# Two graph layers, 32 batches: the product of the score weights ahead of batch 0, and Y of batch 1 directly behind O of batch 0

## The chip, the cores and the metric

The kernel runs on one core of one Trainium2 chip. The metric is the device time of one execution in microseconds; before the change it is 2266.42 us (median of 3 runs, 2264.99 to 2266.43). The engines named below: PE (TensorE, matrix products; PEld is its weight load), DVE (VectorE), ACT (ScalarE), POOL (GpSimd) and SP (SyncE, which issues nearly all DMAs). All arithmetic is fp32.

## The reference

`x` and `adj` are 32 x 512 x 512, `nodemask` 32 x 512, the layer-0 weight W is 512 x 1024, `Wqk` 512 x 1024, `Wv` 512 x 512.

```python
def _L0_gnn_ref(x, adj, W):
    deg = jnp.sum(adj, axis=-1, keepdims=True)
    agg = jnp.einsum('bij,bjf->bif', adj, x) / jnp.maximum(deg, EPS)
    cat = jnp.concatenate([x, agg], axis=2)
    return jax.nn.relu(jnp.einsum('bnf,of->bno', cat, W))

def _L1_gnn_ref(X, adj, mask, Wqk, Wv):
    q, k = jnp.split(X @ Wqk, 2, axis=-1)
    v = X @ Wv
    agg = jnp.einsum('bij,bjd->bid', adj, k * mask[:, :, None])
    w = inv_scale * mask * jnp.einsum('bid,bid->bi', q, agg)
    return jax.nn.softmax(w, axis=1)[:, :, None] * v

h = jnp.maximum(_layernorm(x, axis=-1), 0.0)
x = x + _L0_gnn_ref(h, adj, W)
h = jnp.maximum(_layernorm(x, axis=-1), 0.0)
x = x + _L1_gnn_ref(h, adj, nodemask, Wqk, Wv)
```

## The kernel before

Each batch needs five products of 512 x 512 matrices. Y = h W2 (W2 is the second half of the layer-0 weight) and O = h W1 + A Y, where A is adj divided by its row sums; X1 = x + relu(O) is the input of the second layer. h1 is the normalized X1. U = A (h1 masked), and TV is h1 times two weights at once: T, with the product M = Wq Wk^T (scaled), and V, with Wv. The scores are the row-wise dot products of T and U. M is the same for all batches: it is the "product of the score weights" of the title. Its tiles are called `pm`, its function `multiply`.

Every 512 x 512 product is done by a scheme of seven products of 256 x 256 blocks, m1 to m7 (`product`, L138). The operands are kept in seven slots: four blocks and three sums of blocks, made on DVE by `left_sums` and `right_sums`. One block product is four matmuls (eight passes on PE, since fp32 takes two), PE needs 1.73 us for it. The sums of the result are kept apart in PSUM tiles `pp`, `pr` and `pq`. `pp` takes m1 and is copied by ACT, then m6 is added on top and it is copied again, then m7, a copy, and m4. So m6 cannot start before the copy of m1's block is done, and m7 not before the copy of m6's. The usual order is m1, m2, m6, m5, m7, m3, m4; with `sooner` it is m1, m2, m5, m6, m7, m3, m4.

The order on each engine is written out by hand. `run` (L191) takes one product and a `Plan`: after each block product it issues the functions that the plan has for that step, and then the product's own copies and sums. Each engine works through its own list in this order, and waits at the head of the list.

The operand on the left must lie transposed. For most batches this is done with DMAs: `FrontH.write` (L339, the normalized h) and `FrontA.write` (L377) write a chunk of 128 rows to DRAM (`dhT`, `daT`), `Turned.read` (L311) reads it back in another order (`shT`, `saT`, two halves of four DMAs each), and DVE turns 32 x 32 squares (`Turned.turn`, L314). h1 goes the same way (`dh1T`, `sh1T`). Batch 0 has its h and A transposed on PE instead (`turn_chunk`, L788). The weights, turned on DVE, are w1R (W1's seven slots; `s1` is its raw form), w2R (W2), and wqT and wkT. w1R is written to DRAM once (`dw`, L963, 1.8 MB) and later read slot by slot (`stream`).

SP's DMAs use eight completion semaphores in turn: each DMA waits until the one issued eight before it has landed.

`start` (L829) does batch 0 up to the point where the loop takes over. Before the change its stages on PE are:

1. `spare` (L868): seven matmuls of zeros, after a first Sqrt on ACT that loads its table;
2. batch 0's h, transposed on PE, and Y_0 (`layer0_y(0)`, `sooner`);
3. O_0 (`layer0_out(0, ...)`), with the statistics and writes of h of batch 1, and the turning of Wqk, in its plan;
4. M: `multiply(0)` to `multiply(3)` with no other product beside them (`run(None, 14, p)`, L1035); the plan has what follows from O_0 (`chain`, L807: statistics, normalization, mask and write of h1 of batch 0) and the turns of h of batch 1.

Then the loop runs, for batch i: O_i (not for i = 0), TV of batch i-1, U_i, Y_(i+1). For i = 0 the loop has U_0 and Y_1 alone. So the order on PE is Y_0, O_0, M, U_0, Y_1, O_1, TV_0, U_1, Y_2, O_2 and so on.

Before TV_0 the right operand of TV (`mv`, both M and Wv) gets its own sums of slots: eight functions `weights`, four over rows (`outer`, 1024 wide) and four over columns (`inner`, 1792 wide). Under these names `place` copies a quarter of M or Wv into `mv`.

Of the kernel before, what the change touches and what calls it, by code (L numbers as in the profile page):

```python
# [11 lines left out]
F32 = mybir.dt.float32  # L12
# [10 lines left out]
def kernel(  # L23
# [10 lines left out]

# [166 lines left out]
    def half_rows(t, src, h):  # L226
        for q, rows in enumerate(by_rows(src)):
            nc.sync.dma_start(out=t[q * R:(q + 1) * R, :, :], in_=rows[:, 2 * h:2 * h + 2, :])

    def exchange(src, name, t=None):  # L230


        if t is None:
            t = big.tile([P, 8, P], F32, tag="s", bufs=2, name=name)
        for q in range(Q):
            nc.sync.dma_start(out=t[q * R:(q + 1) * R, :, :], in_=src[:, :, ts(q, P)].rearrange("k r j -> r k j"))
        return t
# [5 lines left out]
    X, AT_, DEG, W, Y, H1M, H1T, U, TV = ({} for _ in range(9))  # L243
# [30 lines left out]

    def first_variance(t):

        mv, rstd, nmr = t
        v, y, r = [small.tile([P, 2], F32, tag=n, name=n) for n in ("first_v", "first_y", "first_r")]
        nc.vector.tensor_scalar(v, mv[:, 0:2, 1], LN_EPS, None, op0=ALU.add)
        nc.scalar.activation(y, v, AF.Sqrt)  # L280
        nc.vector.reciprocal(y, y)
        nc.vector.scalar_tensor_tensor(r, y, -0.5, y, op0=ALU.mult, op1=ALU.mult)
        nc.vector.tensor_tensor(r, r, v, op=ALU.mult)
        nc.vector.scalar_tensor_tensor(rstd[:, 0:2], r, 1.5, y, op0=ALU.add, op1=ALU.mult)
# [38 lines left out]
    class FrontH:  # L323
# [20 lines left out]
        def turn(self, h):  # L344
            self.to.turn(h, hT)

        def sums(self, i):
            left_sums(of(hT))[i]()

    class FrontA:  # L350
# [31 lines left out]
        def turn(self, h):  # L382
            if h == 0:
                AT_[self.b] = slots("aT", 1, f"aT_{self.b}")
            self.to.turn(h, AT_[self.b])
# [82 lines left out]
    def layer0_y(b):  # L468
        y = Y[b] = slots("yh", 1, f"y_{b}")
        return product(f"y_{b}", [(hT, right(w2R))], *into(y), sooner=b == 0)  # L470

    def layer0_out(b, w1):
# [10 lines left out]
        return product(f"o_{b}", [(hT, w1), (AT_[b], right(Y[b]))], place, finish)  # L483
# [282 lines left out]
    def turn_rows(t, h, dst, ordered):  # L766


        t = t.rearrange("p k (a r) -> p k a r", r=R)
        if ordered:  # L770
            for q in range(2):
                o = dst.rearrange("p a (c q r) -> p q c a r", c=C, q=Q)[:, 2 * h + q]
                nc.vector.transpose(o, t[:, q * 4:(q + 1) * 4, :, :])
        else:
            nc.vector.transpose(dst[:, :, ts(h, H)].rearrange("p a (k r) -> p k a r", r=R), t)
# [31 lines left out]
    def chain(p, f, n):  # L807


        def write(c):  # L810
            f.write(c, block(f"h1_{f.b}_{c}"))

        p.at(n(2), f.keep)
        p.at(n(0), f.stats, 2)
        p.at(n(0), shift, f.t, 0, 2)
        p.at(n(0), write, 0)
        p.at(n(1), f.stats, 3)
        p.at(n(1), variance, f.t, 2, 4)
        p.at(n(1), write, 1)
        p.at(n(2), shift, f.t, 2, 4)  # L820
        p.at(n(2), f.mask, 0)
        p.at(n(2), f.mask, 1)
        p.at(n(3), write, 2)
        p.at(n(4), write, 3)
        p.at(n(4), f.mask, 2)
        p.at(n(5), f.masked_sums, 0)
        p.at(n(5), f.mask, 3)

    def start():  # L829
# [6 lines left out]
        room_x(0)  # L836
        s2 = []
        for h in range(2):
            half_rows(X[0][:, 2 * h:2 * h + 2, :], x[0], h)
        for h in range(2):  # L840
            s2.append(exchange(weight_source(w0[:, F:2 * F])[8 * h:8 * h + 8], f"sw2_{h}"))
        fa = FA[0] = FrontA(0)
        fa.load(0)
        fa.load(1)
        room = mv_tile("room").rearrange("p s i a f -> p (s i a f)")
# [4 lines left out]
        w1R = room[:, 0:3584].rearrange("p (s b f) -> p s b f", s=7, b=2)  # L850
        s1 = exchange(weight_source(w0[:, 0:F]), "sw1", rows16(3584))
        fh = FH[1] = FrontH(1)
        for h in range(2):
            fh.load(h, room[:, 9728 + 1024 * h:9728 + 1024 * (h + 1)].rearrange("p (c f) -> p c f", c=2))
        sq = exchange(weight_source(wqk[:, 0:F]), "swq", rows16(5632))
        sk = exchange(weight_source(wqk[:, F:2 * F]), "swk", rows16(7680))
# [7 lines left out]

        nc.scalar.activation(still[:, 0:1], still[:, 1:2], AF.Sqrt)
        spare = mm_tile("spare").rearrange("p a f -> p (a f)")
        for n in range(7):
            nc.tensor.matmul(spare, still[:, 0:P], still, start=True, stop=True)  # L868
# [15 lines left out]
        statistics(X[0][:, 0, :], t, 0, "0_0")  # L884
        statistics(X[0][:, 1, :], t, 1, "0_0")
        first_variance(t)
        shift(t, 0, 2)
        for c in range(2):
            normal(c)
            turn_chunk(v[c], c, "h")  # L890
        for c in range(2):
            keep_chunk(h0, c, "h")
        statistics(X[0][:, 2, :], t, 2, "0_0")
        statistics(X[0][:, 3, :], t, 3, "0_0")
        variance(t, 2, 4)
        turn_right(s2[0], 0, 0, w2R)
        shift(t, 2, 4)
        turn_right(s2[0], 0, 1, w2R)
        for k in range(2):
            turn_right(s2[1], 1, k, w2R)  # L900
        r2, l0 = right_sums(of(w2R)), left_sums(of(h0))

        a0 = AT_[0] = slots("aT", 1, "aT_0")
        rows = {}
# [8 lines left out]
        p.at(0, normal, 2)  # L913
        p.at(0, normal, 3)
# [33 lines left out]
        fb = FA[1] = FrontA(1)  # L948
        p = Plan()
        p.at(0, keep_chunk, a0, 2, "a")  # L950
        p.at(0, turn_chunk, Later(rows, 3), 3, "a")
        p.at(1, keep_chunk, a0, 3, "a")
        p.at(1, fb.load, 0)
        p.at(2, fb.load, 1)
        la = left_sums(of(a0))
        for k in range(4):
            p.at(2 + k // 2, la[k])
        for c in range(C):
            p.at(3 + c, fh.stats, c)
            p.at(7 + c, fh.write, c)  # L960
        p.at(6, variance, fh.t)
        p[7].insert(0, lambda: shift(fh.t))
        p.at(7, lambda: nc.sync.dma_start(out=stream.d.rearrange("s p b f -> p s (b f)"), in_=w1R.rearrange("p s b f -> p s (b f)")))  # L963
        for c in range(C):
            p.at(10 + c, fb.sum, c)
        p.at(7, turn_rows, sq[:, 0:8], 0, wqT, True)
        p.at(8, turn_rows, sq[:, 8:16], 1, wqT, True)
        p.at(9, turn_rows, sk[:, 0:8], 0, wkT, False)
        p.at(9, turn_rows, sk[:, 8:16], 1, wkT, False)
        p.at(10, fh.to.read, 0)  # L970
        p.at(11, fh.to.read, 1)
# [12 lines left out]
        p.at(8, mask_order)  # L984
# [3 lines left out]
        p.at(13, variance, f.t, 0, 2)  # L988
        run(layer0_out(0, right(w1R)), 14, p)


        mv = mv_tile("mv")
        p = Plan()

        def multiply(d):
            m = held["m", d] = mm_tile(f"pm_{d}")
            for a in range(C):
                nc.tensor.matmul(  # L998
# [309 lines left out]
```

## Time and profile before

| what | us |
|---|---|
| runs: lowest, median, highest | 2264.99, 2266.42, 2266.43 |
| span of the profiled execution | 2263.7 |
| batch period in the loop (from one TV to the next) | 69.5 |
| first matmul of `spare`, first needed matmul | 2.28, 11.35 |
| O_0 on PE | 28.15 to 52.77 |
| M on PE | 52.77 to 67.06 |
| U_0 on PE | 67.06 to 79.14 |
| Y_1 on PE | 79.14 to 91.23 |
| O_1 on PE | 91.23 to 115.40 |

The profile is of one execution, on the only core; its span is 2.7 us shorter than the median of the runs. Times in it are microseconds from its first instruction. A line of the timeline gives start, duration, engine, line of the kernel, operation, the tiles written and read, and in brackets how long the engine had been idle before and what ended that. A line of the busy times by stretch gives the stretch, then for PE, PEld, DVE, ACT and POOL the busy time and the number of instructions, the granted clock, the DMA share and GB/s. DMA issues are shown on the queue that issues them, and their landing is a separate figure.

### The profile page before, as it was taken

To read this page: it belongs to the slowest core of one execution; us is meant where nothing else is said; L and a number is where in the kernel's file an instruction comes from. 1 tells how busy PE (TensorE), PEld (TensorE's weight loads), DVE (VectorE), ACT (ScalarE), POOL (GpSimd) and SP (SyncE) were. 2 spreads that over 40 slices of the span, in tenths; PEclk is the share of its full clock that TensorE was granted. 3 is DMA by queue.
4 is the path that set the end of the run, shared out by engine and by line. 5 is a ranking of instruction groups with operands and counts; after the bars stand their busy time and mean duration, and the time that the engine had idled before them with its cause. 6 is when DMAs were issued, how large, how long until landed. Compare 5 with 4: busy or idle time off the path is not lost.

```text
span 2263.7 us, 32771 instructions
## 1 busy us (share of the span) xinstructions
PE 2256.1 (100%) x10498; PEld 1976.5 (87%) x10498; DVE 1913.3 (85%) x3782; ACT 1028.4 (45%) x1898; POOL 175.3 (8%) x260
## 2 busy tenths in 40 slices
PE   9999999999999999999999999999999999999999
PEld 7888888888888888888888888888888888888888
DVE  7788888888888888888888888888888888888776
ACT  4454543445434544344444344543454443445323
POOL 0000000000000000100000000001000000000000
PEclk9999999999999999999999999999999999999999
DMA  9978787887878787877878788887878787887644
GB/s 220 246 218 241 208 210 191 206 229 212 210 198 199 210 229 200 209 192 208 233 203 207 194 204 220 219 209 200 192 213 229 202 208 195 204 233 205 155 124 108
DMA packets 409644, 463.68 MB, mean 205 GB/s; under 512 B 37856, under 2 KB 271328, under 8 KB 405248
## 3 DMA queue, kind: packets, MB, share of 16 engines
q1 hardware_dynamic: 399904, 428.56, 70.1%
q0 software_dynamic: 8928, 32.51, 8.6%
q8 instruction: 83, 1.36, 0.3%
q14 instruction: 89, 0.73, 0.1%
q10 hardware_dynamic: 640, 0.52, 0.1%
HBM read 293.93 MB, written 167.51 MB: 204 GB/s over the span
## 4 chain that ended last, share of the span: by engine, by line
PE 99%; DMA 0%; DVE 0%; ACT 0%; SPq 0%; POOL 0%; issue 0%; DVEq 0%; POOLq 0%
PE ptv L502 28%; PE pp_o L129 19%; PE pp_y L129 10%; PE pp_u L129 10%; PE pq_o L129 9%; PE pq_u L129 5%; PE pq_y L129 5%; PE pr_o L129 5%; PE pr_y L129 2%; PE pr_u L129 2%; PE pw L553 1%; PE pm L998 1%; PE spare L868 0%; DMA n<-in_x_dram 0%; PE pp_v L129 0%; PE pp_t L129 0%
## 5 line engine op out<-in xcount | busy, mean ns | idle before, releaser
L502 PE MATMUL ptv<-mv,h1T 128*128 128x256 f32 x2940 | 639.8, 379 | 0.1
L502 PEld LDWEIGHTS ptv<-mv,h1T 128*128 128x128 f32 x2940 | 558.4, 190 | 76.6 <-DVE xu L481 0.7
L100 DVE TENSOR_TENSOR tv<-tv 128x256 f32<-128x256 f32 (+1 forms) x644 | 320.9, 510 | 13.1 <-ACT tv L106 1.5
L106 ACT ACTIVATE tv<-ptv 128x512 f32<-128x512 f32 (+1 forms) x360 | 185.0, 541 | 260.0 <-PE ptv L502 259.4
L129 PE MATMUL pp_y<-wide 128*128 128x256 f32 x1024 | 242.1, 379 | 0.9 <-ACT y L106 0.7
L129 PE MATMUL pp_u<-h1m,aT 128*128 128x256 f32 x1024 | 241.9, 379 | 0.0
L129 PE MATMUL pp_o<-y,aT 128*128 128x256 f32 x1024 | 241.9, 379 | 0.0
L129 PE MATMUL pp_o<-w,wide 128*128 128x256 f32 x992 | 234.3, 379 | 0.0
L129 PEld LDWEIGHTS pp_y<-wide 128*128 128x128 f32 x1024 | 194.3, 190 | 27.9 <-ACT y L106 1.1
L129 PEld LDWEIGHTS pp_u<-h1m,aT 128*128 128x128 f32 x1024 | 194.5, 190 | 26.8 <-issue 0.5
L129 PEld LDWEIGHTS pp_o<-y,aT 128*128 128x128 f32 x1024 | 194.5, 190 | 26.4
L129 PEld LDWEIGHTS pp_o<-w,wide 128*128 128x128 f32 x992 | 188.5, 190 | 25.6
L106 ACT ACTIVATE o<-pp_o 128x512 f32<-128x512 f32 x96 | 57.3, 597 | 300.4 <-PE pp_o L129 300.4
L106 ACT ACTIVATE y<-pp_y 128x512 f32<-128x512 f32 x128 | 76.4, 597 | 236.1 <-PE pp_y L129 234.9
L100 DVE TENSOR_TENSOR tv<-ptv,tv 128x512 f32<-128x512 f32 x240 | 139.6, 613 | 43.2 <-PE ptv L502 39.5
L103 DVE TENSOR_TENSOR h1T<-h1T 128x512 f32<-128x512 f32 (+1 forms) x189 | 163.4, 878 | 1.2
L106 ACT ACTIVATE xu<-pp_u 128x512 f32<-128x512 f32 x127 | 75.8, 597 | 191.9 <-PE pp_u L129 191.9
L273 POOL TENSOR_TENSOR rstd<-rstd,mhalf 128x2 f32<-128x2 f32 (+1 forms) x96 | 78.6, 818 | 647.7 <-DVE rstd L272 645.6
L129 PE MATMUL pq_u<-h1m,aT 128*128 128x256 f32 x512 | 121.1, 379 | 0.0
L129 PE MATMUL pq_y<-wide 128*128 128x256 f32 x512 | 121.0, 379 | 0.0
L129 PE MATMUL pq_o<-y,aT 128*128 128x256 f32 x512 | 120.9, 379 | 0.0
L100 DVE TENSOR_TENSOR tv<-ptv,m_tv 128x512 f32<-128x512 f32 (+1 forms) x120 | 72.1, 622 | 56.2 <-PE ptv L502 55.3
(152 smaller groups left out, 3258.9 us busy)
## 6 DMA issues: line engine op xcount, KB each, us to landing
w<-dw SPq DMA_DIRECT2D x217, 256.0 KB, 4.2
a<-in_adj_dram SPq DMA_DIRECT2D x256, 128.0 KB, 3.0
dx<-xu SPq DMA_DIRECT2D x32, 1024.0 KB, 5.0
sh1T<-dh1T SPq DMA_DIRECT2D x256, 128.0 KB, 3.3
shT<-dhT SPq DMA_DIRECT2D x248, 128.0 KB, 5.7
daT<-a SPq DMA_DIRECT2D x124, 256.0 KB, 3.0
saT<-daT SPq DMA_DIRECT2D x248, 128.0 KB, 3.3
xu<-in_x_dram SPq DMA_DIRECT2D x124, 256.0 KB, 5.4
```

Of the source, the lines that this page charges most:

```text
L100: (on or nc.vector).tensor_tensor(o, a, b, op=ALU.add)
L103: (on or nc.vector).tensor_tensor(o, a, b, op=ALU.subtract)
L106: nc.scalar.activation(o, i, AF.Copy)
L129: nc.tensor.matmul(p[:, rc, :], lt[:, LEFT[k], dk, ts(rc, P)], right[:, dk, :], start=first and rc == 0 and dk == 0, stop=True, skip_group ...
L273: nc.gpsimd.tensor_tensor(rstd[:, a:b], rstd[:, a:b], mhalf[:, a:b], op=ALU.pow)
L502: nc.tensor.matmul(banks[n][:, :, ts(i, P)], left[:, LEFT[k], LEFT_IN[j], :], mvR[:, RIGHT[k], RIGHT[j], :, :], start=first and i == 0, st ...
L553: nc.tensor.matmul(banks[n][:, ts(i, P)], left[:, LEFT[k], LEFT_IN[j], :], mvR[:, RIGHT[k], RIGHT[j], which, :], start=first and i == 0, s ...
L998: nc.tensor.matmul(m.rearrange("p a f -> p (a f)"), wqT[:, a, ts(d, P)], wkT[:, a, :], start=(a == 0), stop=(a == C - 1),)
```

## The change

- M is computed at the start, ahead of batch 0. Wq and Wk are the first loads, Wq in four pieces of 256 KB (64 KB for each DMA), Wk in two of 512 KB; x of batch 0 and W2 follow. These loads are issued alternately from SP and ACT (`two_queues`). `multiply` works on half rows (256 wide).
- `spare` has five matmuls instead of seven, and the first Sqrt on ACT and `first_variance` (which used Sqrt) are gone: the variances of batch 0 go to POOL as all others do.
- Y_1 runs directly behind O_0, with `sooner`; U_0 follows Y_1. Both move into `start`, and the loop begins with i = 1. The order on PE is M, Y_0, O_0, Y_1, U_0, O_1, TV_0 and so on.
- h of batch 1 gets its own room (`HT[1]`), in `tv`, which is unused until TV_0; w1R lies in the other half of `tv`, and Y_1 takes w1R's place once O_0 is done. A of batch 1 takes A of batch 0's buffer: its first half is turned during U_0, the second in O_1.
- The plans of these stages are written anew: in O_0 the statistics of batch 1's x come one step earlier, all four writes of its h come at steps 6 and 7, the read back at steps 8 and 9, the turns at 10 and 11; the placing of Wv and the turning of the mask are in O_0; what `chain` had spread over M's fourteen steps is in the first five of Y_1's seven. Loads and writes of adj of batch 1, x of batch 2 and adj of batch 2 move with their stages.

```diff
+        exchange(wk_rows[0:8], "swk_0", sk[:, 0:8], two_queues)
+        for d in range(C):
+            exchange(wq_rows[d], f"swq_{d}", sq[:, 4 * d:4 * d + 4], two_queues)
+        exchange(wk_rows[8:16], "swk_1", sk[:, 8:16], two_queues)
         room_x(0)
+        for h in range(2):
+            half_rows(X[0][:, 2 * h:2 * h + 2, :], x[0], h, two_queues)
...
-        nc.scalar.activation(still[:, 0:1], still[:, 1:2], AF.Sqrt)
         spare = mm_tile("spare").rearrange("p a f -> p (a f)")
-        for n in range(7):
+        for n in range(5):
...
+        for d in range(C):
+            multiply(d, 0)
+        multiply(0, 1)
+        place_m(0)
         for c in range(2):
             normal(c)
+        multiply(1, 1)
+        place_m(1)
+        multiply(2, 1)
+        for c in range(2):
             turn_chunk(v[c], c, "h")
         for c in range(2):
             keep_chunk(h0, c, "h")
+        multiply(3, 1)
...
-        return product(f"y_{b}", [(hT, right(w2R))], *into(y), sooner=b == 0)
+        return product(f"y_{b}", [(HT.get(b, hT), right(w2R))], *into(Y[b]), sooner=b < 2)
...
         for c in range(C):
-            p.at(3 + c, fh.stats, c)
-            p.at(7 + c, fh.write, c)
-        p.at(6, variance, fh.t)
-        p[7].insert(0, lambda: shift(fh.t))
+            p.at(2 + c, fh.stats, c)
+            p.at(6 + c // 2, fh.write, c)
+        p.at(5, variance, fh.t)
+        p[6].insert(0, lambda: shift(fh.t))
         p.at(7, lambda: nc.sync.dma_start(out=stream.d.rearrange("s p b f -> p s (b f)"), in_=w1R.rearrange("p s b f -> p s (b f)")))
+        p.at(7, mask_order)
+        p.at(8, mask_turn)
+        p.at(9, mask_keep)
+        p.at(8, fh.to.read, 0)
+        p.at(9, fh.to.read, 1)
         for c in range(C):
+            p.at(8 + c, lambda c=c: place(c, 1, wvN[:, c, :]))
             p.at(10 + c, fb.sum, c)
-        p.at(7, turn_rows, sq[:, 0:8], 0, wqT, True)
-        p.at(8, turn_rows, sq[:, 8:16], 1, wqT, True)
-        p.at(9, turn_rows, sk[:, 0:8], 0, wkT, False)
-        p.at(9, turn_rows, sk[:, 8:16], 1, wkT, False)
-        p.at(10, fh.to.read, 0)
-        p.at(11, fh.to.read, 1)
+        p.at(10, fh.turn, 0)
+        p.at(11, fh.turn, 1)
+        for k in range(4):
+            p.at(11 + (k + 1) // 2, fh.sums, k)
         f = F1[0] = FrontH1(0)
         p.at(12, f.stats, 0)
         p.at(12, f.stats, 1)
         p.at(13, variance, f.t, 0, 2)
+        p.at(13, weights[0])
         run(layer0_out(0, right(w1R)), 14, p)
+        Y[1] = w1R
         p = Plan()
+        p.at(0, f.stats, 2)
+        p.at(0, shift, f.t, 0, 2)
+        p.at(0, write, 0)
+        p.at(0, f.stats, 3)
+        p.at(0, variance, f.t, 2, 4)
+        p.at(1, write, 1)
+        p.at(1, shift, f.t, 2, 4)
+        p.at(1, f.keep)
+        p.at(1, f.mask, 0)
+        p.at(1, f.mask, 1)
+        p.at(2, write, 2)
+        p.at(2, write, 3)
+        p.at(2, weights[1])
+        p.at(3, f.mask, 2)
+        p.at(3, f.mask, 3)
...
+        p.at(5, fb.write, 0)
+        p.at(5, fb.write, 1)
...
+        run(layer0_y(1), 7, p)
+        fh = FH[2] = FrontH(2)
+        p = Plan()
+        p.at(0, fb.write, 2)
+        p.at(0, fb.write, 3)
+        p.at(0, f.turn, 0)
+        p.at(1, f.turn, 1)
+        for n in range(4):
+            p.at(0, stream.load)
+        p.at(1, fb.to.read, 0)
+        p.at(2, fh.load, 0)
+        p.at(2, fh.load, 1)
+        p.at(3, fb.to.read, 1)
+        p.at(3, load_x, 1)
...
+        for c in range(C):
+            p.at(3 + c, fh.stats, c)
+        p.at(4, fb.turn, 0)
...
+        run(layer1_u(0), 7, p)
...
+            if i == 1:
+                p.at(0, FA[1].turn, 1)
+                for k in (0, 2):
+                    p.at(0, FA[1].sums, k)
```

## The prediction

> **What bounds the kernel now.** I read the page's engine shares and chain first, then the timeline of PE at the start, the busy times by stage, the timeline around the hand-over from one stage to the next, and last the landing times of single DMAs.
>
> ```profile
> PE 2256.1 (100%) x10498; PEld 1976.5 (87%) x10498; DVE 1913.3 (85%) x3782; ACT 1028.4 (45%) x1898; POOL 175.3 (8%) x260
> ...
> PE 99%; DMA 0%; DVE 0%; ACT 0%; SPq 0%; POOL 0%; issue 0%; DVEq 0%; POOLq 0%
> ```
>
> TensorE (PE) is the chain. There are two places where time can be won: PE time that does no needed work, and gaps. The timeline of PE shows both at the very start:
>
> ```profile
> 2.28 9.23 PE L868 MATMUL spare<-late 128*128 128x512 f32 x14 [2.28 <-ACT late L865]
> 11.35 1.04 PE L792 MATMUL h<-late,h 128*128 128x128 f32 x8
> 12.63 1.99 PE L129 MATMUL pp_y<-wide 128*128 128x256 f32 x8 [0.25 <-ACT wide L106]
> ...
> 21.55 1.99 PE L129 MATMUL pp_y<-wide 128*128 128x256 f32 x8 [0.69 <-ACT y L106]
> ```
>
> The first needed matmul starts at 11.35; `spare` multiplies zeros. The 0.69 at 21.55 is m7 waiting until ACT has copied m6's sum out of the same PSUM tile, because `sooner` puts m6 directly in front of m7. The waits of PE from 12 to 130 us are these 0.25 and 0.69 alone. By stage (PE, PEld, DVE, ACT, POOL):
>
> ```profile
> 28.15:52.77 24.62, 24.62 (x119) 21.68 (x118) 20.48 (x38) 9.32 (x19) 1.02 (x1) 1.00 1.13 245
> 52.77:67.06 14.29, 14.29 (x38) 6.32 (x37) 8.54 (x20) 8.65 (x14) 1.39 (x2) 1.00 0.85 278
> ...
> 91.23:115.40 24.17, 24.17 (x113) 21.28 (x112) 23.89 (x32) 8.26 (x18) 0.00 (x0) 1.00 0.69 182
> ```
>
> These are O_0, the weight product `pm`, and O_1. In the middle one DVE works 8.54 of 14.29: this product is the cover under which the hand-over from O_0 to U_0 runs (statistics of X1, its normalization, the transposed h of batch 1). O_1 has no room on DVE. What runs under that cover:
>
> ```profile
> 46.51 0.40 SPq L963 DMA_DIRECT2D dw<-room  x1
> ...
> 54.68 1.52 ACT L294 ACTIVATE h<-xu,nmr,rstd 128x512 f32<-128x512 f32 x2 [4.47 <-DVE nmr L288]
> ...
> 55.84 4.02 SPq L236 DMA_DIRECT2D shT<-dhT  x8
> ...
> 63.02 1.25 DVE L316 STREAM_TRANSPOSE wide<-shT 128x1024 f32<-128x1024 f32 x1 [1.48 <-DMA shT<-dhT]
> ```
>
> h of batch 1 is ready in hT only at 64.3, 11.5 us after O_0's end, and nobody minds: Y_1 starts at 79.14. DVE waits for both `shT` halves (this is the second), ACT's first write of X1's h waits 4.47 for DVE's shift. The time from issue to landing of `dw`, and then of the `dhT` write behind it (issued at 47.01), each asked for alone:
>
> ```profile
> DMA to landing us min/median/max: 7.3/7.3/7.3
> ...
> DMA to landing us min/median/max: 8.8/8.8/8.8
> ```
>
> So `dw` (1.8 MB) lands at 53.85, and a 256 KB write issued 0.5 us after it lands at 55.8: it queues behind it. The `dhT` write issued before `dw` lands at 45.91 + 3.7 = 49.6, so `dw` moves for 4.2 us.
>
> **What the Trainium skill says.** (1) "DMA: Bandwidth & Descriptors", section "Queues, rings and completion order": each DMA engine consumes descriptors in ring order, SP and ACT have rings on the same 16 engines. The trace agrees (dw and dhT above), so two issuing queues save issue time but no transfer time. (2) "TensorE: Matmul & The Clock Gate", Part 1: the array runs at half clock until about one busy window has passed. Here: `spare` passes come every 0.855 us until 8.3, then every 0.43, 6.0 us after the first. (3) Same page, section "Architectural detail": the queues of ACT and DVE are strictly first in, first out; both timelines agree. (4) "ScalarE: Activation LUTs", "What ACT_TABLE_LOAD costs": about 1283 ns; the trace has 1.28 at 0.73.
>
> **The change part by part.**
>
> *Head.* Without the Sqrt, `spare` waits for DVE's memset, done at 1.42, and starts at 1.45 instead of 2.28. Five matmuls are ten passes: 7 at 0.855 and, after 6.0 us, 3 at 0.43: end 8.75. The weights come first now. In the trace the first of the 128 KB loads lands at 0.73 + 2.1 = 2.9 and the sixteenth at 7.88 + 4.7 = 12.6: 0.65 us per 128 KB. Wqk (2 MB) is then in at about 12.7, x at 17.5, W2 at 22.5, a at 27.5, s1 at 33. Each piece of Wq is turned about 1.5 us before its matmuls, so PE runs from 8.75. `pm` costs the same 32 passes (13.85 = 14.29 less 0.43 of mask transposes): eight half groups of 1.73, plus 0.87 for the first h transposes: Y_0 starts at 8.75 + 13.85 + 0.87 = 23.5. ACT must be in time: its last DMA issue waits for x (17.3), then 0.45, table load 1.28, place 0.6, two normals 1.6: 21.25, and the transpose of chunk 1 is due at 21.35. Just enough; a later ACT costs its lateness. Y_0 at 12.63 plus 13.85 would be 26.5: **3.0 gained**. Bounds: clock change a microsecond earlier or later, weights 1 to 3 later: 0 to 3.7. Y_0's further inputs all move by about 10 us as the PE does.
>
> *Hand-over, on the clock of before (O_0 at 28.15).* Wqk's turns (4.84 of DVE) leave O_0; its DMA no longer stands before wvN and adj of batch 1. Statistics come a step earlier but behind DVE's same queue, so shift ends at 41.0. ACT normalizes four chunks, 0.8 each, to 44.1. The four `dhT` writes go out as they come; the last is issued at 44.15 and lands 2.0 later (an unqueued `daT` write needs 2.0), at 46.2. `dw`, issued at 44.5, follows for 4.2: 50.4. Both `shT` reads queue behind it, 8 x 0.65: the halves land at 53.0 and 55.6. PE finishes O_0 at 52.77 + 0.43 = 53.2 and now wants them.
>
> But Y_1's start is not what ends last. On ACT, write(0) of X1 stands in front of the copy of Y_1's first block, and m6 (and with `sooner` m7) reuses that PSUM tile. write(0) needs shift of X1, and on DVE these stand before it: second turn 1.25, sum 0.65, O_01's two 1.42, two sums 1.3, two statistics 1.74, sum 0.65, variance 0.2, weights[0] 1.2, O_10 0.7, statistics 0.85, shift 0.15: 10.1, from 55.6. With write 0.8 and copy 0.6, m6 may start at 67.1 instead of 58.4. From that copy to the copy of m6's block ACT has write(1) 0.76, two masks 1.33, two writes 1.52, m5's copy 0.6, two masks 1.33, the copy 0.6: 6.15, so m7 at 73.3. Three blocks of 1.727: U_0 at 78.5. Without waits Y_1 (12.09, from 53.2) would end at 65.3: **13.2 lost**. Bounds: if the reads don't queue behind dw, DVE starts the turns at 48.2 (end of O_11's pair) and U_0 starts at 48.2 + 1.25 + 10.1 + 1.4 + 6.15 + 5.2 = 72.3: 7.0 lost; with a slower tail of dw, 15.
>
> *U_0, O_1.* SP has adj writes of batch 1, which wait for ACT behind Y_1's last copy, then 1 MB of w, saT, then x of batch 2. The last are about 12 us of queue behind Y_1's end, and DVE's statistics of x stand in front of the turn of aT that O_1 needs. From there DVE works without a pause to O_1's last xu add: 32.4 us by the rows of before (9.6 up to the aT sums, 8.3 for h1T and O_00, 14.8 for weights, O_11, O_01, statistics), 0.3 before O_1's start. In before that add starts at
>
> ```profile
> 119.42 0.68 DVE L481 SCALAR_TENSOR_TENSOR xu<-pp_o,xu 128x512 f32<-128x512 f32 x1
> ```
>
> and ends 28.9 after O_1's start, when the second product of TV wants its PSUM tile; 32.1 is **3.3 lost** (0 to 6). From batch 2 on, both kernels are the same.
>
> *Edits with one answer.* w1R, then Y_1, and h of batch 1 lie in tv, unused until TV_0: same shapes, no cost. first_variance (Sqrt) gives way to POOL's power (0.25 + 0.74 after the variance), under `pm`. wvN's placings (0.6 each) go from U_0 into O_0, where ACT is busy 9.32 of 24.62; the mask's transposes (0.43 of PE) move too. aT of batch 1 shares aT_0's buffer: its first turn runs beside U_0, its second (1.25, two sums 1.3) comes after it, and is in O_1's sum above. If ACT's slack in O_0 were gone, the dhT writes would slip by as much.
>
> Sum: -3.0 + 13.2 + 3.3 = +13.5. The profiled execution spans 2263.7, the runs' median is 2266.4, 2.7 more; the same distance after: 2277.2 and **2280 us**.
>
> **The rivals.** A: the reads pass dw, or land early; DVE and ACT order alone remain: -3.0 + 7.0 + 3.3 = +7.3, 2274; with nothing lost in O_1, 2270. For it: the four dhT writes themselves are quick. Against: the 8.8 us landing. B, faster: the hand-over stays hidden and only the head counts: -3.0, 2263.4. It decides if X1's shift ends by 57.0 (m5's end 58.4 less write and copy); even with reads at once I get 48.2 + 1.25 + 10.1 = 59.6, so a quarter of DVE's queue would have to be off. C: Wqk in 64 KB pieces, eight in flight, arrives late, the head wins nothing, and O_1's lag goes on into TV: +18 to 19, 2285. That PE's work itself grows or shrinks is excluded: the same passes are issued, less four of `spare`.
>
> **How the numbers follow.** Forecast (+9 to +16) 0.56; A 0.25; C 0.13; B 0.06. The range 2270 to 2286 holds the forecast, A and most of C. A measurement tells about 0.2% (4.5 us) from no change: faster 0.05, same 0.04 (A's edge and B's), slower 0.91.
>
> **What would show it.** `pm` from about 8.75 and Y_0 near 23.5 for the head; `shT` landing after dw; a wait of PE at the m6 and one at the m7 of Y_1, both put down to ACT's copy of y, of some 9 and 4.5 us; DVE busy through O_1 and a wait at TV_0's second product. It is wrong if Y_1 runs without these waits, or if `pm` waits for its weights.

## The result, and the profile after

The changed kernel takes 2287.65 us (median of 4 runs, 2286.13 to 2288.65) beside 2265.7 (4 runs, 2264.81 to 2266.43) for the kernel before on the same chip: a ratio of 1.0097, 95% interval 1.0083 to 1.0112. The forecast, 2280, had the direction and fell 7.6 us short; the range ended at 2286. The profiled execution spans 2284.8, 21.1 more than before.

The shares of the chain that ended last (the work that set the end of the run) are no longer PE alone; before, PE had 99%.

```profile
PE 94%; DMA 3%; DVE 1%; ACT 0%; issue 0%; SPq 0%; POOL 0%; DVEq 0%; ACTq 0%
```

The timeline of PE at the start of the changed kernel, for the head:

```profile
1.48 7.29 PE L823 MATMUL spare<-late 128*128 128x512 f32 x10 [1.48 <-DVE late L784]
8.61 12.66 PE L843 MATMUL pm<-late 128*128 128x256 f32 x56
21.71 1.36 PE L763 MATMUL h<-late,h 128*128 128x128 f32 x8 [0.44 <-ACT h L835]
22.91 1.89 PE L843 MATMUL pm<-late 128*128 128x256 f32 x8
24.64 1.89 PE L103 MATMUL pp_y<-wide 128*128 128x256 f32 x8
```

M runs from 8.61 on, and Y_0 starts at 24.64. Before it started at 12.63; with M's 13.85 in front that would be 26.48, so the head gains 1.84. O_0 follows without loss and ends at 65.32, where it ended at 52.77. The busy times by stage of the changed kernel, for O_0, Y_1, U_0, O_1 and TV_0 (PE, PEld, DVE, ACT, POOL, then granted clock, DMA share, GB/s):

```profile
39.99:65.32 25.33, 25.33 (x122) 21.72 (x120) 13.25 (x26) 11.32 (x24) 1.01 (x1) 1.00 0.74 201
65.32:92.68 27.36, 17.66 (x57) 13.94 (x57) 19.04 (x36) 8.63 (x14) 2.47 (x3) 0.75 0.58 149
92.68:104.77 12.09, 12.09 (x58) 10.64 (x56) 5.96 (x7) 4.12 (x7) 0.00 (x0) 1.00 0.92 243
104.77:137.27 32.50, 26.78 (x113) 22.09 (x112) 29.45 (x44) 10.90 (x21) 1.01 (x1) 0.95 0.89 201
137.27:158.43 21.16, 21.16 (x100) 18.62 (x99) 20.64 (x45) 15.29 (x27) 2.40 (x3) 1.00 0.80 241
```

Two stages lost time: Y_1 takes 27.36 instead of 12.09, and O_1 32.50 instead of 24.17. In both PE is busy less than the stage lasts, and in Y_1 even the busy time is 17.66, where the same work took 12.09: the granted clock is 0.75. The waits of PE say for what (waiter, releaser, total, times, longest):

```profile
PE pp_y L103 <- ACT tv L80: 6.7, 2, 4.9
PE pp_o L103 <- ACT o L80: 3.6, 2, 2.3
PE pp_y L103 <- DVE tv L283: 3.0, 1, 3.0
PE pp_o L103 <- DVE aT L283: 2.2, 1, 2.2
```

The first and third lines are Y_1 (its output lies in `tv`): ACT's copies before m6 and m7, and the turn of h of batch 1 on DVE. The others are O_1. On the timelines of PE, DVE and ACT in Y_1 the chain can be followed:

```profile
68.34 3.68 PE L103 MATMUL pp_y<-wide,tv 128*128 128x256 f32 x8 [3.02 <-DVE tv L283]
71.85 1.90 PE L103 MATMUL pr_y<-wide,tv 128*128 128x256 f32 x8
...
80.41 3.78 PE L103 MATMUL pp_y<-wide,tv 128*128 128x256 f32 x8 [4.93 <-ACT tv L80]
85.94 3.46 PE L103 MATMUL pp_y<-wide,tv 128*128 128x256 f32 x8 [1.75 <-ACT tv L80]
```

```profile
69.54 1.25 DVE L283 STREAM_TRANSPOSE tv<-shT 128x1024 f32<-128x1024 f32 x1 [1.25 <-DMA shT<-dhT]
...
78.90 0.13 DVE L255 SCALAR_TENSOR_TENSOR nmr<-mv,rstd 128x2 f32<-128x2 f32 x1
```

```profile
79.06 0.81 ACT L261 ACTIVATE h<-xu,nmr,rstd 128x512 f32<-128x512 f32 x1 [16.47 <-DVE nmr L255]
79.78 0.57 ACT L80 ACTIVATE tv<-pp_y 128x512 f32<-128x512 f32 x1
```

ACT stood idle for 16.47 us at the head of its list, behind which lay a copy whose data was ready after m1; DVE reached `nmr` (the shift of X1's normalization) only after the turn, and the turn waited for its reads. The three slow blocks take 3.46 to 3.78 us where a block at full clock takes 1.9 (blocks at full clock start 1.73 apart, since the end of one overlaps the start of the next).

### The profile page after: what moved, and what is told of

It reads as the page before. It is cut to its first block, busy times and chain, and to the rows that moved or that the text cites. A ratio compares the mean times of both kernels' runs of the same rounds, so it can differ in the third digit from the quotient of the medians.

```text
span 2284.8 us, 32852 instructions
## 1 busy us (share of the span) xinstructions
PE 2262.3 (99%) x10526; PEld 1985.8 (87%) x10526; DVE 1912.4 (84%) x3778; ACT 1025.0 (45%) x1895; POOL 176.6 (8%) x261
## 4 chain that ended last, share of the span: by engine, by line
PE 94%; DMA 3%; DVE 1%; ACT 0%; issue 0%; SPq 0%; POOL 0%; DVEq 0%; ACTq 0%
PE ptv L470 28%; PE pp_o L103 18%; PE pp_u L103 9%; PE pp_y L103 9%; PE pq_o L103 9%; PE pq_u L103 5%; PE pq_y L103 5%; PE pr_o L103 5%; PE pr_u L103 2%; PE pr_y L103 2%; PE pw L521 1%; DMA w<-dw 1%; DMA mv<-in_L_gnn_Wqk_dram 0%; DMA a<-in_adj_dram 0%; DMA mv<-in_L_gnn_W_dram 0%; DMA dw<-tv 0%
## 5 line engine op out<-in xcount | busy, mean ns | idle before, releaser
L74 DVE TENSOR_TENSOR tv<-tv 128x256 f32<-128x256 f32 (+1 forms) x645 | 321.5, 510 | 13.2 <-ACT tv L80 1.5
L103 PE MATMUL pp_y<-wide 128*128 128x256 f32 x992 | 234.4, 379 | 0.7 <-ACT y L80 0.7
L103 PE MATMUL pp_o<-y,aT 128*128 128x256 f32 x992 | 234.4, 379 | 0.0
L103 PE MATMUL pp_o<-w,wide 128*128 128x256 f32 x960 | 226.8, 379 | 0.0
L103 PEld LDWEIGHTS pp_y<-wide 128*128 128x128 f32 x992 | 188.3, 190 | 26.6 <-ACT y L80 1.1
L103 PEld LDWEIGHTS pp_o<-y,aT 128*128 128x128 f32 x992 | 188.3, 190 | 25.6
L103 PEld LDWEIGHTS pp_o<-w,wide 128*128 128x128 f32 x960 | 182.4, 190 | 24.8
L103 PE MATMUL pq_y<-wide 128*128 128x256 f32 x496 | 117.3, 379 | 0.0
```

The costliest lines, as they stand in the source:

```text
L74: (on or nc.vector).tensor_tensor(o, a, b, op=ALU.add)
L103: nc.tensor.matmul(p[:, rc, :], lt[:, LEFT[k], dk, ts(rc, P)], right[:, dk, :], start=first and rc == 0 and dk == 0, stop=True, skip_group ...
```

## The experiments

The table has the kernels in which order or load was changed; times by stage are from one profile each, and the stretch is from O_0's end to O_2's start. Without M, PE has 94.0 us of work in it, by the stages of the kernel before. The rows come from several chips, on which the medians of the kernel before lie 1.1 us apart. In b2 to b4, O_0 itself takes 27.0 to 27.4 us instead of 25.3, ahead of the stretch.

| run | median us | Y_1 | O_1 | TV_0 | stretch |
|---|---|---|---|---|---|
| before | 2264.6 to 2265.7 | 12.1 | 24.2 | 21.3 | 108.3 with M |
| before without M | 2264.9 | 12.1 | 24.6 | 21.2 | 108.2 |
| after | 2287.65 | 27.4 | 32.5 | 21.2 | 117.3 |
| a1, dw early | 2281.25 | 20.6 | 34.0 | 21.2 | 111.9 |
| a2, waits filled | 2286.67 | 25.2 | 33.2 | 21.2 | 115.8 |
| a3, cover put back | 2286.54 | 26.9 | 33.7 | 21.2 | 118.0 |
| b1, ScalarE's order | 2278.33 | 14.6 | 37.0 | 21.2 | 109.0 |
| b2, front of x early | 2282.54 | 20.1 | 33.6 | 21.2 | 111.1 |
| b3, with O_1 | 2283.39 | 19.8 | 31.0 | 21.2 | 111.3 |
| b4, sums on GpSimd | 2284.23 | 15.5 | 35.2 | 21.4 | 112.9 |
| c2, O_1 alone | 2287.59 | 26.6 | 25.5 | 27.8 | 116.6 |
| c1, all orders | 2277.68 | 12.9 | 28.1 | 27.6 | 107.9 |
| d1, degrees later | 2281.87 | 12.9 | 29.6 | 21.2 | 111.7 |
| f1, A_1 early | 2276.24 | 12.9 | 33.7 | 23.2 | 107.2 |
| g1, batch 2 later | 2281.56 | 13.0 | 25.4 | 25.3 | 110.4 |

**The place of M is free before.** The edit of the first run takes M out of the kernel before, the second puts sixteen idle matmuls where M was:

```diff
-            p.at(3 * d, multiply, d)
-            p.at(3 * d + 3, lambda d=d: place(d, 0, held["m", d].rearrange("p a f -> p (a f)")))
+            p.at(3 * d + 3, lambda d=d: place(d, 0, wvN[:, d, :]))
```

```diff
+            for _ in range(n):
+                nc.tensor.matmul(r, w2R[:, 0, 0, 0:P], w2R[:, 0], start=True, stop=True, skip_group_check=True)
...
+        return product(f"y_{b}", [(HT.get(b, hT), right(w2R))], *into(Y[b]), sooner=b < 2, filler={(1, 0): 16} if b == 1 else {})
```

> The kernel before with the product M left out of its place between O_0 and Y_1 (the score weights are then taken from Wv, so scores and output differ; what is left out is M's 16 matmuls of 512 columns, 13.85 us of TensorE). Theory H (the hand-over to Y_1 is as long as M): only 2 to 5 us less than before, 2261 to 2264, and a wait of 9 to 12 us in front of or within Y_1. Rival W (M's time on TensorE is what that place costs): 13.5 to 14 us less, 2252.

> The changed kernel with 16 idle matmuls (13.8 us of TensorE, results unused) between O_0 and Y_1, where the product M stood before. The output is the same; nothing is left out. Theory H (the hand-over from O_0 to Y_1 takes as long as M did, whatever TensorE does in it): adding 13.8 us of matmuls costs nothing, total 2285 to 2288, since Y_1's first two waits vanish and m6, m7 and U_0 come when they came, at full clock. Rival W (TensorE's work is the bound there, the waits are a side effect of the order in which blocks are fed): 2298 to 2301, all 13.8 us added.

Without M the kernel before takes 2264.9 us: ratio 1.0001 (0.9993 to 1.0010). 13.85 us of matmuls less gain nothing, less even than the 2 to 5 us of theory H. The wait is in front of and within U_0, not Y_1 as expected (in that kernel U_0 follows O_0), and the waits of PE are 9.3 us:

```profile
PE pp_u L129 <- ACT h1m L418: 7.0, 1, 7.0
PE pp_u L129 <- DVE h1m L103: 2.3, 1, 2.3
```

The remaining 4.4 us are slow passes, at a clock of 0.74 in the stretch from O_0's end to U_0's:

```profile
51.93:78.10 26.17, 16.94 (x61) 13.69 (x61) 16.42 (x33) 14.75 (x25) 1.39 (x2) 0.74 1.01 301
```

(busy 16.94, for 12.1 of U_0 and 0.4 of mask turns at full clock). And with 13.8 us of matmuls added to the changed kernel the time is 2286.54, 1.1 under it. Both halves of the reason hold: M cost nothing where it was, and what stood under it needs its time with or without M. (That the gain is nothing to a tenth of a microsecond is partly luck: 9.3 of the 13.7 us are waits for the hand-over, the rest is the clock that fell with them.) In front of batch 0 M costs 12.55: O_0 ends at 65.32 instead of 52.77. So the change could only win if the stretch behind O_0 shrank by as much; it grew by 9.0.

**The reads behind dw.**

```diff
-        p.at(7, lambda: nc.sync.dma_start(out=stream.d.rearrange("s p b f -> p s (b f)"), in_=w1R.rearrange("p s b f -> p s (b f)")))
+        p.at(3, lambda: nc.sync.dma_start(out=stream.d.rearrange("s p b f -> p s (b f)"), in_=w1R.rearrange("p s b f -> p s (b f)")))
```

> The changed kernel with w1's copy to DRAM (dw) issued at step 3 of O_0's plan instead of step 7. Theory Q (the reads of Y_1's left operand stand behind dw on SP's queue and DMA engines, so the whole wait of Y_1 moves with them): the reads land near 60.5 and 62.6 instead of 66.97 and 69.42, Y_1 ends 6 to 8.5 us earlier, total about 2280 (2279 to 2282), 6 to 8 us under the changed kernel. Rival R (the wait is set by VectorE's and ScalarE's order alone, the transfer is hidden anyway): the reads land earlier and Y_1 takes its 27 us all the same, total 2287 to 2288. A result between (2 to 4 us gained) would say that the engines' order takes over half way.

2281.25, ratio 1.0072 (1.0056 to 1.0089) against the changed kernel's 1.0097: 6.4 us lower (5.7 by the ratios), theory Q. The time of the `shT` reads from issue to landing (min, median, max), in the changed kernel and in this run:

```profile
DMA to landing us min/median/max: 5.2/6.4/8.0
```

```profile
DMA to landing us min/median/max: 2.5/3.2/3.6
```

Y_1 gained 6.8 us, and O_1 gave 1.4 back. Y_1 keeps 6.6 us of waits for ACT.

**The clock.** Idle matmuls fill the waits of Y_1 and O_1.

```diff
+        return product(f"y_{b}", [(HT.get(b, hT), right(w2R))], *into(Y[b]), sooner=b < 2, filler={(1, 0): 3, (6, 0): 5, (7, 0): 2} if b == 1 else {})
...
+        return product(f"o_{b}", [(HT.get(b, hT), w1), (AT_[b], right(Y[b]))], place, finish, filler={(1, 1): 2, (6, 0): 1, (4, 0): 2} if b == 1 else {})
```

> The changed kernel with idle matmuls of w2's sums by themselves, 0.86 us each, results unused, in the waits of Y_1 (3 before the first block's start, 5 before m6, 2 before m7) and of O_1 (2 before the second half of m1, 1 before m6, 2 before m4). The output is the same; nothing is left out. Theory C (the clock gate slows the blocks behind each wait, and part of that is on the path): the waits end at the same times, the blocks behind them run at full speed (1.7 us instead of 3.2 to 3.5), granted clock of Y_1 near 1.0 instead of 0.75, total 3 to 4 us lower, about 2284. Rival 1 (all 8.2 us of slow passes are on the path): 8 us lower, about 2279.5. Rival 2 (the slow blocks wait for something else than the clock, or are the records' error): slow blocks stay, total 2287 to 2290.

Y_1's clock is 1.00 and its blocks run at full speed, so the slow passes are the clock's. Y_1 is 2.2 us shorter, but O_1 0.7 longer (its clock is still 0.95), and the median is 1.0 under the changed kernel, less than the measurement can tell from nothing. Y_1 had 5.6 us of slow passes, and only those 2.2 came off with them; theory C's 3 to 4 us in the total was too much.

**ScalarE's order, VectorE's load.** b1 keeps dw early and puts Y_1's copies ahead of the normalizations of h1. b2 has the front of x of batch 1 three steps earlier, dw behind its reads, and four of the eight weight sums in O_0. b3 adds an order for O_1 (reads of A_1 ahead of x of batch 2, statistics in O_1). Of b1's edit:

```diff
-        p.at(0, write, 0)
...
-        p.at(1, write, 1)
...
+        p.at(3, write, 0)
+        p.at(3, write, 1)
```

> The kernel with dw at step 3, and ScalarE's order in Y_1 changed: Y_1's own copies (c11, m5, c12, c22) stand ahead of the normalisations and masks of H1_0 that wait for VectorE. Output as before, nothing left out. Theory E (with the reads early, what is left of Y_1's wait is ScalarE held by nmr ahead of the copies): m6 starts with no wait, m7 is held only by the first two normalisations (about 73.7 instead of 78.4 on the clock of the dw run), Y_1 ends 4 to 5 us earlier, total about 2277 (2276 to 2278.5). Rival V (VectorE's queue is the limit and the order on ScalarE is nothing): Y_1's waits go to m7 or to the start of U_0 and the total stays 2280 to 2282.

> The kernel with the whole front of x of batch 1 three steps earlier in O_0 (statistics, writes, reads, turn, sums), dw behind its reads, the first four weight sums in O_0, and ScalarE's order in Y_1 as copies first. Output as before, nothing left out. Theory V (VectorE is nearly full in the hand-over: 19.0 us of work in Y_1's 27.4, which cannot fit in 12.1): with some 9 us of it moved into O_0, where VectorE is busy only half the time, Y_1 takes 13 to 15 us, total 2272.5 to 2275. Rival E (ScalarE's order was all): no better than the run with that order alone, 2276 to 2278. Rival D (something in front of the masks of H1_0 that neither order touches): Y_1 shortens and U_0 waits as long, 2278 or more.

> The same as the run with the early front of x, and in O_1: the reads of A_1's transpose and of x1 ahead of the loads of x of batch 2, the turn of A_1 ahead of the statistics of that x, which move into O_1, the row sums of A_2 behind O_1's copies. Output as before, nothing left out. Theory (O_1 lost its 8 us to engines queued behind late loads, not to TensorE or to DMA capacity): O_1 takes 25 to 28 us instead of 32 to 34, total another 4 to 7 us lower, 2267 to 2270. Rival (VectorE's 29.5 us of work in O_1 is itself the bound): O_1 stays near 30 and TV_0 or U_1 takes over the rest, only 1 to 3 us lower, 2271 to 2273.

b1: 2278.33. Y_1 falls from 20.6 to 14.6, more than theory E asked, but only half of it stays, since O_1 goes from 34.0 to 37.0; its wait for A_1's turn is now 7.0:

```profile
PE pp_o L103 <- DVE aT L283: 7.0, 1, 7.0
```

That turn stands on DVE behind statistics of x of batch 2, whose last load lands 2.6 us earlier than in a1 (99.3 and 101.9), while O_1 starts 5.5 earlier. b2 (2282.54, outside all its theories' numbers) has the first normalizations in front of m5's copy on ACT, and m6's copy stands behind that, so m7 waits 5.9. Y_1 is no better than in a1, and the run decides nothing about VectorE. b3 (2283.39, also outside) removes the wait for A_1's turn, leaves one of 1.8 for its sums, and makes one of 4.9 for ACT's m5 copy, behind the normalizations of x of batch 2.

**GpSimd for the weight sums.** The eight `weights` go to the idle engine.

```diff
-        weights = [right_sums(outer)[k] for k in range(4)] + [right_sums(inner)[k] for k in range(4)]
+        weights = [right_sums(outer, nc.gpsimd)[k] for k in range(4)] + [right_sums(inner, nc.gpsimd)[k] for k in range(4)]
```

> The same as the run with both orders, and the eight sums of the score and value weights (about 13 us of VectorE) on GpSimd, which stands idle there. Output as before, nothing left out. Theory V (VectorE is what O_0 to O_1 are short of): 1 to 4 us lower than with both orders, about 2266. Rival (GpSimd takes two to three times as long for each sum and slows VectorE beside it, and TV_0 waits for the last sums): 2 to 15 us higher, TV_0 starts late. No run here shows such a sum on GpSimd, so both ends are open.

2284.23, 0.8 above b3 and hardly to be told from it, where 12.8 us of DVE were to be saved. The timelines of POOL and DVE in this run:

```profile
76.41 7.95 POOL L77 TENSOR_TENSOR mv<-mv 128x1792 f32<-128x1792 f32 x2
```

```profile
76.67 3.75 DVE L337 TENSOR_SCALAR deg<-deg 128x2 f32<-128x2 f32 x1
...
80.54 4.36 DVE L74 TENSOR_TENSOR tv<-m_y,tv 128x512 f32<-128x512 f32 x1
```

One of the two sums takes 4.0 us on GpSimd (2.0 on DVE). The first DVE operation takes 3.75 instead of 0.16 and ends at 80.42, where GpSimd's first sum ends (half of its 7.95 us). DVE's sum takes 4.36 instead of 0.69 and ends at 84.90, 0.5 us behind GpSimd's second. The Trainium skill says so in "SBUF — State Buffer", section "SBUF: two separate sides": the two share a port pair that one instruction holds to its end. The trace agrees, with the times just given.

**All orders, and O_1's alone.** c1 is dw early, the copies and the first half's `nmr` first in Y_1, and O_1's order; c2 has O_1's order alone, on the changed kernel.

> dw at step 3 of O_0, in Y_1 ScalarE's copies first and nmr of the first half first on VectorE, one weight sum fewer in O_0's end; in U_0 the reads of A_1's transpose and of x1 ahead of the loads of x of batch 2, the turn of A_1 ahead of that x's statistics; in O_1 the normalisations of x of batch 2 behind O_1's m5 copy, the loads and row sums of A_2 behind those. Output as before, nothing left out. Theory (the 21 us are three queues each holding ready work behind late work: SP's dw ahead of Y_1's reads, ScalarE's nmr wait ahead of Y_1's copies, VectorE's and ScalarE's waits for x of batch 2 ahead of O_1's turn and copies): Y_1 near 14 us, U_0 12.1, O_1 25 to 27, total 2267 to 2270. Rival (the stretch is short of VectorE time: 67.7 us of work for 73 us of TensorE): the waits move on to U_0, TV_0 or U_1 and the total stays at 2274 to 2278, near the run with dw and ScalarE's order.

> The changed kernel with U_0's and O_1's orders alone edited (reads of A_1 and x1 ahead of the loads of x of batch 2, turn of A_1 ahead of its statistics, normalisations of that x behind O_1's m5 copy, loads and row sums of A_2 behind those); Y_1 and dw as in the changed kernel. Output as before, nothing left out. Theory: Y_1 stays at 27 us, O_1 falls from 32.5 to 25 to 27, total 5.5 to 7.5 us lower, 2280 to 2282. Rival (O_1's waits follow from Y_1's lateness): O_1 stays over 30, total 2285 to 2288.

c2: O_1 falls from 32.5 to 25.5, as expected, and TV_0 rises from 21.2 to 27.8: 2287.59, nothing won. Its total misses the theory's 2280 to 2282; the loss now stands at TV_0's second product. c1: Y_1 is down to 12.9, but the same wait of 4.7 us appears in TV_0. DVE's timeline of c1 shows it:

```profile
127.68 0.17 DVE L337 TENSOR_SCALAR deg<-deg 128x2 f32<-128x2 f32 x1 [4.27 <-ACT a L333]
...
128.02 0.68 DVE L449 SCALAR_TENSOR_TENSOR xu<-pp_o,xu 128x512 f32<-128x512 f32 x1
```

The degrees of A_2 wait for ACT's row sums of the late-loaded A_2, and O_1's last add (the second line), on which TV_0 waits, stands behind them. Median 2277.68: 10 us won, 12.4 still missing. The total is the rival's (2274 to 2278), so c1 alone does not tell the order of late data from a lack of DVE time.

**Mending that one too.** d1 moves the degrees, sums and writes of A_2 into TV_0, the loads of batch 3 behind them, and reads A_1 ahead of three loads of w.

> The run with all orders edited, and two edits more: the degrees of A_2, which wait for its late row sums on ScalarE, no longer stand ahead of O_1's last sum on VectorE (row sums, degrees and writes of A_2 lie in TV_0, the loads of batch 3 behind them), and the reads of A_1's transpose stand ahead of three of the four loads of w. Output as before, nothing left out. Theory (each time a queue holds ready work behind late work, the wait is made there and moves when that one is mended): TV_0 falls from 27.6 to about 21.3, O_1 from 28.1 to 25 or 26, total 7 to 9 us lower than with the orders alone, 2268.5 to 2271. Rival (VectorE is short of time in this stretch): the wait shows up again in TV_0 or U_1 and the total falls less than 3 us, 2275 to 2278.

TV_0 is 21.2 again, but U_1 takes 23.2 instead of 12.1 (waits 6.1 and 2.2): on ACT, the normalizations of x of batch 3 stand ahead of a copy and wait 9.8 us. 2281.87, worse than c1: the wait moved on as the rival said, and the total lies above even the rival's 2275 to 2278.

**VectorE's capacity.** All this can mean that DVE lacks time: from O_0's end to Y_2 it has 82 us of work in c1, and PE 82 at full clock. Three runs leave the eight weight sums out (GpSimd fills zeros in their place).

```diff
+        weights = [(lambda s=s, k=k: nc.gpsimd.memset(s(k), 0.0)) for s in (outer, inner) for k in (4, 6, 5, 1)]
```

> The kernel with all orders (dw early, Y_1, U_0 and O_1) with the eight sums of the score and value weights left out: GpSimd fills their blocks with zeros in the same places instead, so the scores and the output differ; VectorE has 12.8 us less to do between O_0 and TV_0. Theory V (VectorE is short of time there): 5 to 10 us lower than with all orders, 2268 to 2273. Rival Q (the waits are made by late loads in front of ready work, whatever VectorE's load): 0 to 2 us lower, 2275.5 to 2278.

> The changed kernel with the same eight sums left out and filled with zeros by GpSimd. Theory V: Y_1 loses the 3.7 us of sums that stand in VectorE's queue before the masks' sums, O_1 the 6 us before its degrees; 4 to 8 us lower than the changed kernel, 2280 to 2284. Rival Q: Y_1's waits are set by the reads behind dw and by ScalarE's order and do not move, 0 to 2 us lower, 2285.5 to 2288.

> The kernel before with the same eight sums left out and filled with zeros by GpSimd. Both theories: TensorE waits for nothing there but 0.7 us in Y_0, so nothing is gained, 2264 to 2266; it is the control for the other two. If it falls by over 1 us, the sums were on the path before as well and the comparison is void.

2278.48 (c1 had 2277.68), 2286.60 (the changed kernel 2287.65), and 2265.50 for the control. Ten us of DVE's work less in the same 94.4 us from O_0's end (81.6 busy in c1, 71.7 without the sums) and no gain where theory V asked for 5 to 10: it falls for c1. The test is not quite clean, since in e1 two small DVE operations beside GpSimd's filling take 3.4 us instead of 0.3. In e2, Y_1 does fall by 3.2 us, near theory V's 3.7, but O_1 takes 34.0 instead of 32.5 with 5.7 us less of DVE's work in it, and the median falls by 1.0 only: in the total, DVE's capacity is not what the changed kernel lacks. What is left is the order of late data; that is argued from the waits, as no order tried here removes them all.

**The order of transfers.** In c1 the DMA share is 0.39 from 66 to 78 us, and 0.96 and 1.13 in the two stretches of 12 us behind:

```profile
66.00:78.00 12.00, 11.31 (x52) 9.62 (x52) 10.02 (x25) 6.85 (x11) 1.56 (x3) 1.00 0.39 154
78.00:90.00 12.00, 11.59 (x54) 9.89 (x53) 9.46 (x12) 5.99 (x11) 0.00 (x0) 1.00 0.96 285
90.00:102.00 12.00, 9.57 (x45) 8.11 (x44) 11.75 (x15) 1.19 (x2) 0.00 (x0) 1.00 1.13 230
```

f1 takes A_1's round trip (degrees, writes, reads) from behind Y_1 into O_0's end and Y_1, and reads h1 of batch 0 after it; g1 also normalizes x of batch 2 behind O_1's copies, and moves what waits for batches 2 and 3 further back.

> The kernel with all orders, and A_1's row sums, degrees, writes and reads moved from behind Y_1 into O_0's end and Y_1, where the DMA engines are less than half busy; H1_0's transposed reads come after A_1's turn, in O_1; the degrees of A_2 in TV_0. Output as before, nothing left out. Theory T (transfers crowded into U_0 and O_1 make the waits left in O_1 and TV_0): O_1 takes 24.5 to 26 us instead of 28.3, TV_0 21.3 to 23 instead of 27.8, total 2266 to 2271. Rival (the waits move on once more): one of TV_0, U_1 or Y_2 takes over, total 2275 to 2280.

> The run with A_1's round trip in Y_1, and: the normalisations of x of batch 2 behind O_1's last copy, the row sums, degrees and writes of A_2 behind TV_0's first copies, the statistics of x of batch 3 at TV_0's end, its normalisations and the row sums of A_3 in U_1 and Y_2. Output as before, nothing left out. Theory (order alone makes the waits, none is a lack of any engine or of the DMA's rate): O_1 24.5 to 26 us instead of 33.9, TV_0 and U_1 without waits over 1 us, total 2265 to 2269, the kernel before within 0.2 per cent. Rival (the waits move on once more, to U_1, Y_2 or O_2): 2272 to 2277.

f1: 2276.24, the lowest of the versions with M in front, but by its ratio, 1.0054 (1.0040 to 1.0068), no better than c1 with 1.0055. The wait for A_1's turn is 1.0 where c1 had 2.4, and 5.5 us go to m5's copy behind the normalizations. g1 mends this (O_1 25.4), and loses it in TV_0, U_1 (16.7) and Y_2 (17.9): 2281.56. Both totals miss their theory. No version here beats the kernel before.

## Why the prediction was wrong, and where it was right

*The direction and the hand-over: right.* M was read as "the cover under which the hand-over runs", and a3 and a4 show it as plainly as can be. dw ahead of the reads, `nmr` behind DVE's list, ACT's copies behind `nmr`, waits at m6 and m7: all in the trace. The two waits were forecast as some 9 and 4.5 us and are 4.9 and 1.75, because 3.0 us of waiting lie ahead of m1 and m1 and m6 run slowly. On the clock of before (11.84 earlier), m6 starts at 68.6 for 67.1, m7 at 74.1 for 73.3, U_0 at 80.8 for 78.5: 15.3 lost for 13.2. Rival A (reads pass dw) is excluded by a1 and by the trace (dw lands at 64.22, the first read at 64.94), rival B by the result. Rival C named the nearest total, 2285, by luck: its reasons did not happen, as the head won 1.84 and TV_0 lost nothing.

*Sizes in it.* dw's transfer was put at 4.2, and from the landing of the last `dhT` write (58.15) to its own (64.22) it takes 6.1: 2.0 late. From issue to landing it took 7.8, near the 7.3 of before, which would have been the better figure to carry over. DVE's list came out shorter (9.5 for 10.1). Not in the sum was the clock: I had cited the half clock for `spare` and not asked what PE's own waits would do to it. m7's block takes 1.5 us more for it, on the path; a2 puts the clock at about 1 us of the total, no more than the noise.

*The head: right mechanism, too large.* 1.84 instead of 3.0. M starts at 8.61, near the 8.75 forecast. Then `pm` does wait for its weights, one of the signs of being wrong, but for 0.4 us only (the second half of Wk is turned at 15.77). ACT costs 0.9: x lands about a microsecond later than forecast, so that ACT's table load begins at 19.07 and the transposes of h wait for it. The first load lands at 4.48, not 2.9. The profiles of the other kernels with this head have Y_0 at 23.9 to 25.0.

*O_1: the step that failed.* "From there DVE works without a pause to O_1's last xu add" gave a term of 3.3, with the loss at TV_0's second product. (Its three parts, 9.6, 8.3 and 14.8, add up to 32.7 and not 32.4, so it should have been about 3.5.) Measured are 8.3, all inside O_1, none in TV_0: 5.0 of the 7.6 us missing. The hand-over's 2.1 and the head's 1.2 are the rest, less 0.7 by which other stages came out shorter. PE's waits in O_1, and ACT's:

```profile
108.82 3.24 PE L103 MATMUL pp_o<-tv,aT 128*128 128x256 f32 x8 [2.16 <-DVE aT L283]
...
117.19 1.99 PE L103 MATMUL pp_o<-w,tv 128*128 128x256 f32 x8 [1.24 <-ACT o L80]
...
133.72 1.99 PE L103 MATMUL pp_o<-w,tv 128*128 128x256 f32 x8 [2.32 <-ACT o L80]
```

```profile
115.85 0.81 ACT L261 ACTIVATE n<-n,nmr,rstd 128x512 f32<-128x512 f32 x1 [10.28 <-DMA w<-dw]
116.57 0.57 ACT L80 ACTIVATE o<-pp_o 128x512 f32<-128x512 f32 x1
...
132.46 0.63 ACT L333 ACTIVATE a<-a 128x512 f32<-128x512 f32 x1 [1.34 <-DMA shT<-dhT]
...
133.09 0.58 ACT L80 ACTIVATE o<-pp_o 128x512 f32<-128x512 f32 x1
```

The sum had only DVE's work in it and put ACT's list at nothing. DVE was indeed busy without a pause, from 105.8 to 132.2, but that is not what PE waited for alone. On ACT the normalizations of x of batch 2 stand idle for 10.28 us ahead of m1's copy: they need `nmr`, which DVE writes at 115.61, after statistics of an x whose last load landed at 107.80 (the profile names a DMA as the releaser). A row sum of A_2 waits for its load, which lands at 132.39, ahead of the copy before m4. These two cost waits of 1.24 and 2.32. The wait for A_1's turn (2.16), behind the same statistics, halves the clock of the blocks behind it. Waits of 5.7 and slow passes of 2.6 make the 8.3. c2 shows that the lists' order made them: with it changed, O_1 takes 25.5, and the loss moves to TV_0's second product, where the forecast had it. And e2 shows that the amount of DVE's work did not set O_1's end: with 5.7 us of it taken out, O_1 is no shorter.

*What stays open.* Whether an order exists that brings the stretch well below c1's 107.9 us. Each order of the later runs took away the wait that it named, and another appeared behind it. In g1, DVE is busy without a pause from 103 us through O_1's end, and TV_0 waits 1.3 us for a weight sum, so its work may bind there as it did not in c1; this was not tried. The books of c1 are simple: its stretch is as long as that of the kernel before with M in it (107.9 and 108.3), so the 12.4 us still missing are about the 12.55 that M costs in front. PE's 94.0 us of work is the floor of the stretch; a kernel that reached it would be 14 us below c1, about where the kernel before is. So by these figures even a perfect order could win little.

## What to carry to other kernels

A product that PE does while others hand over is free there; before moving it, take it out and measure: if nothing is won, its new place is a pure cost, and the old place needs other work. Where order is written by hand, walk each engine's list, ACT's as well as DVE's, and ask at each waiting instruction what ready work stands behind it: that is where a wait is made. A wait taken away is won only if the next late datum comes earlier too, so look at the stage behind before counting the gain.

## What the runs showed of the hardware

- How short a wait of PE halves its clock: the Trainium skill ("TensorE: Matmul & The Clock Gate", Part 1) has half clock after an idle window of about 3.4 us. Over all traces here, waits up to 1.65 us did not bring it; of those from 1.7 to 2.4 some were followed by blocks at half clock (2.16 in O_1 of the changed kernel, 2.30 in c2), and others of the same length were not (2.38 in e2); of those of 2.7 and more all but two were (3.10 in a1, 3.31 in b4). So the figure is no safe bound. Half clock lasted 3 to 6 us as a rule, and 8.7 where a second wait fell into it (1.75, before m7 of Y_1).
- A DVE sum of 128x512 took 4.36 us instead of 0.69 beside a GpSimd sum, and a DVE operation on 128x2 took 3.75 instead of 0.16 in the same run: with sums on GpSimd, DVE's busy time did not fall (83.8 beside 83.0 in the stretch from O_0's end to Y_2).
